# Layer 0 of a two-layer transformer kernel: a second place for queries and keys in transit, and one experts' product to a slot

## The chip, the core and the metric

The kernel runs on one core of one Trainium2 chip. The core has a matrix engine (TensorE, PE in the profile, with its weight loads shown apart as PEld), a vector engine (VectorE, DVE), a scalar engine (ScalarE, ACT), a general engine (GpSimd, POOL), and a queue for transfers (SyncE, SP). Each engine runs its own instructions in the order in which the program has them and waits for the others through semaphores. The metric is the device time of one execution in microseconds (us). The kernel before took 1177.23 us, the median of three runs (1175.32 to 1181.05).

## The reference, cut to what matters

Four sub-layers follow one another on 2048 tokens of width 256, each as `x = x + f(layernorm(x))`, all in float32.

```python
def _L0_attn_ref(x, w_project, w_out):        # 16 heads of 16, 4 sequences of 512, causal
    q, k, v = ...                             # einsum('bsd,od->bso', x, w_project)
    att = softmax(where(causal, -1e9, q @ k.T / 4))
    return einsum('bsd,od->bso', att @ v, w_out)

def _L0_ffn_ref(h, router_w, router_b, expert_w, expert_b):
    logits = (h @ router_w.T + router_b).reshape(T, O, E)         # O = 256, E = 8
    w, sel = top_k(softmax(logits), 2);  w = w / sum(w)
    c = zeros((T, E)).at[t_idx, sel].add(w)                       # 256 choices fall on 8 experts
    expert_out = einsum('th,eoh->teo', h, expert_w) + expert_b
    return einsum('te,teo->to', c, expert_out)
```

The second layer has an attention with 16 heads of 128 over the sequences' position in the batch, and a gated network of width 2048 with 4-bit weights. For this change the experts' layer is the part to keep in mind: per group of 128 tokens it needs four products of 128x256 by 256x512 for the router (the logits), then a long chain on DVE that turns the logits into the eight weights `c` of each token, and then four products of the same size with the experts' matrices (the results), which ACT scales by `c` and DVE adds up. There are 16 groups, so 64 logit products and 64 result products.

## The kernel before

Tokens are cut into 16 groups of 128, four groups to a block (`NBLK` = 4). Layer 0's attention runs over the blocks in turn, because of the causal mask: block j sees the keys of blocks 0 to j. Its work is cut into 44 batches (`batches`, filled at the head of the attention): 4 batches for block 0, 8 for block 1, 16 for block 2 and 16 for block 3. A batch n does, on PE: the scores of the next batch (`greatest`, L647), the transpose of the row maxima (`shift`, L676), a mask (`mask`, L660), then the product with the values for the batch before (`mixed`, L731) and the scores once more, transposed (`powers`, L695), for the exponentials on ACT. DVE takes the maxima (L666) and subtracts them from the queries (L679).

All instructions of PE, DVE, ACT and POOL are in an order written by the program. Everything that isn't the attention itself is put between these steps by a small planner. A job is a generator, a `Stream`, that says before each piece what it needs: an engine, a cost in planned us, a gap in slots and a condition. A call of `fill` opens a slot. It sets what is left of each engine's budget to `min(left, 0) + budget`, so that a debt is carried on and a rest is thrown away, and then goes through the streams in order and lets each put in pieces as long as `ready` says yes. `ready` asks for `left > 0`, so a piece may overdraw the budget. Batch n has slots 2n+1 (after `mask`) and 2n+2 (after `powers`), with PE budgets of 2.0 and 2.4 for blocks 0 and 1, 1.8 and 2.2 for block 2, 1.6 and 2.0 for block 3; DVE gets 2.6 in each.

The streams that matter here, in the order in which a slot asks them:

- `prepare(j)` (j = 2, 3): normalises a block, transposes it, and runs `projections(j, xT)`: the values (cost 1.75), then for each half of the 256 query and key columns two calls of `project`, i = 0 for the keys and 1 for the queries, at 1.75 each. `project` multiplies (L545), ACT copies the product into a tile `stage` (L549), and after i = 1 eight DMAs from SP (L555) carry the stage's rows to their places in `qk`. The tile `stage` is in pool `a1`, which has one buffer for that name.
- `divided(j, s)`: the attention's division and output product (L749, L766, L778); once a block's last is done, `hidden_pieces(j)` makes the experts' normalised input `xT`.
- `addition_pieces` (DVE 1.55: adds half a group's results to the residual), `total_pieces` and `weight_pieces` (17 DVE pieces for a group, 18 planned us; when the last is done, the group enters `weights`).
- `result_pieces` and, after it, `logit_pieces`: each piece is one product, PE cost 1.85. Conditions tie them to `made()`, the number of groups whose 17 DVE pieces are done, in fractions: logit g, pair p waits for `made() >= g - 0.9 + 0.22 p` and for the weights of group g - 2; result h, pair p for `made() >= h + 1 + 0.22 p` or for no logits waiting. The third and fourth product of a group wait until the sum of the first two has been added.

The experts' tiles are in pools with one buffer per name (`b1`): among them `hi4` and `lo4` (the weights' chain) and `part` (a half group's scaled results). Before the first group's chain starts, `hi4` holds the biases as they were loaded (`bs`), and `part` holds what the biases are folded in with (`rows`, last read by the fold at L252).

What of the experts' work is left at the end of layer 0's attention goes on in layer 1's attention. There 16 steps p (block j, key head kv) have nine slots each. Until step 8 (`LAST`), a step gets `share = products_left / (9 * (LAST + 1 - p))`, and its slots have a PE budget of `1.9 * share + 0.2` and a DVE budget of `2.7 * share + 1.4`. From step 9 on `share` is 0. Ahead of step 10 a loop of slots (PE 2.0, DVE 3.0) runs until the last sum is added; from step 10 the 4-bit weights of layer 1's gate and up matrices are unpacked in the space that this frees (`weight_in_pieces`, L878 to L905).

Of the kernel before, what the change touches and what calls it, by code (L numbers as in the profile page):

```python
# [8 lines left out]
F32 = mybir.dt.float32  # L9
# [7 lines left out]
P = 128  # L17
# [15 lines left out]
def tile_transformer(  # L33
# [71 lines left out]
    b1 = w_ffn0.enter_context(tc.tile_pool(name="f0_1", bufs=1, side="right"))  # L105
# [6 lines left out]
    slot = 0  # L112

    def need(engine, cost, gap=0, cond=None):
        return engine, cost, gap, cond

    class Stream:
# [4 lines left out]
        def ready(self, left):  # L122
            if self.next is None:
                return False
            engine, cost, gap, cond = self.next
            return left[engine] > 0 and slot >= self.last + gap and (cond is None or cond())

        def go(self):
            engine, cost = self.next[:2]
# [17 lines left out]
    left = {"PE": 0.0, "DVE": 0.0}  # L147
# [113 lines left out]
    logits, weights, halves = {}, {}, {}  # L261
# [187 lines left out]
    with ExitStack() as l0:  # L449
# [90 lines left out]
        def project(j, xT, half, stage, i):  # L540

            at = 256 * (1 - i) + 128 * half
            ps = ps_dn.tile([P, 512], F32, tag="dn", name=f"qk_ps{j}_{half}_{i}")
            for hc in range(2):
                nc.tensor.matmul(  # L545
                    ps, lhsT=wp[:, hc, at : at + P],
                    rhs=xT[:, hc].rearrange("p s q -> p (s q)"), start=hc == 0, stop=hc == 1,
                )
            nc.scalar.copy(stage[:, i], ps)  # L549
            if i:  # L550
                to = 4 + j % 2
                for r in range(8):
                    h = 32 * (r % 4)
                    eng = nc.scalar if j == 0 and r % 2 else nc.sync
                    eng.dma_start(  # L555
                        out=qk[h + 4 : h + 20, 2 * half + r // 4, j : to + 1 : to - j].rearrange(
                            "p i s q -> p i (s q)"
                        ),
                        in_=stage[16 * r : 16 * r + 16],
                    )  # L560

        def values(j, xT, s):

            ps = ps_dn.tile([P, 2, HID], F32, tag="dn", name=f"v_ps{j}_{s}")
            for i in range(2):
                for hc in range(2):
                    nc.tensor.matmul(
                        ps[:, i], lhsT=xT[:, hc, s + i], rhs=wp[:, hc, 512:768],
                        start=hc == 0, stop=hc == 1,
                    )  # L570
            at = j * per_block
            to = va[:, at : at + per_block].rearrange("p (s h d) -> p s h d", s=NS, d=17)
            nc.scalar.copy(
                to[:, s : s + 2, :, 0:16], ps.rearrange("p s (h d) -> p s h d", d=16)
            )
# [14 lines left out]
        def projections(j, xT):  # L590
            if j > 1:
                for s in (0, 2):
                    yield need("PE", 1.75, 1, cond=lambda: blanked > 5 * j - 10)
                    values(j, xT, s)
            for half in range(2):
                if j or half:
                    stage = a1.tile([P, 2, 512], F32, tag="stage", name=f"stage{j}_{half}")
                else:
                    stage = unused("stage0", "p (i q) -> p i q", i=2)
                for i in range(2):  # L600

                    yield need(
                        "PE", 1.75, 0 if half or i else 1,
                        cond=lambda: j < 2 or done >= 8 * j - 12 and blanked >= 5 * j - 5,
                    )
                    project(j, xT, half, stage, i)
                if half == (not j) and j < 2:
                    for s in (0, 2):
                        yield need("PE", 1.75)
                        values(j, xT, s)  # L610

        def prepare(j):

            out = []
            yield from norm_pieces(
                j, b1, b2, out, cond=lambda: j == 2 or inputs[2].next is None
            )
            xT = a1.tile([P, 2, NS, P], F32, tag="xT0", name=f"xT0_{j}")
            yield from inputs_T(j, out[0], xT)
            yield from projections(j, xT)  # L620

        def unused(name, pattern, **sizes):

            tile = b2.tile([P, NE, HID], F32, tag="lg", name=name)
            return tile.rearrange("p e o -> p (e o)")[:, :1024].rearrange(pattern, **sizes)
# [188 lines left out]
        for piece in projections(0, xT):  # L814
            pass
# [3 lines left out]
        greatest(0)  # L819
        mask(0)  # L820
        inputs = {1: Stream(projections(1, xT))}
        done = blanked = 0
        fold = Stream(fold_pieces())
# [4 lines left out]
        for n in range(NBT):  # L828
            j, s, gs = batches[n]
# [92 lines left out]
    with ExitStack() as l1:  # L922
# [198 lines left out]
        for p in range(-1, NP):  # L1121
            j, kv = divmod(p, NKV)
# [179 lines left out]
```

## Time and profile before

| | |
|---|---|
| median of the runs | 1177.23 us |
| the profiled execution, its own time | 1182.05 us |
| its span, first to last instruction | 1180.3 us |
| PE, PEld, DVE, ACT, POOL busy | 1148.1, 663.9, 809.7, 484.3, 108.1 us |
| layer 0's attention, from the first batch to the last | about 31 to 404 us |
| layer 1's attention | about 404 to 840 us |
| the gated network | about 840 to 1180 us |

A row of the timeline has the start of an instruction (or of several alike in a row), its length, engine and line, what it writes and reads, its shape, and in brackets how long the engine was idle ahead of it and who ended that. A row of the windows has the length of a stretch and then the busy time and the number of instructions of each engine in it, the clock that was granted to TensorE as a share of full speed, the share of the DMA engines' time and GB/s. Matmuls are pipelined, and the end of each is modelled, so two that follow one another overlap in the rows: four matmuls of 128x512 are shown with 0.59 us each but start 0.43 us apart, and a product takes 1.72 us from its start to the next.

### The profile page before, as it was taken

How to read it: one execution, taken by the hardware profiler on the slowest of the kernel's cores; microseconds unless marked ns; L12 is line 12 of the kernel's file. 1: busy time of each engine (PE TensorE's matmuls, PEld its weight loads, DVE VectorE, ACT ScalarE, POOL GpSimd, SP SyncE). 2: the span in 40 equal slices, each digit the busy share in tenths (PEclk: the TensorE clock that was granted, in tenths of full speed). 3: DMA queues.
4: the chain of work that ended last, by engine and by line, in shares of the span. 5: the costliest groups of instructions: out<-in, count | busy, mean ns of one | idle time of the engine just before them, and what ended most of it. 6: DMA issues, size and time to landing. Idle time of an engine off the chain costs nothing.

```text
span 1180.3 us, 18580 instructions
## 1 busy us (share of the span) xinstructions
PE 1148.1 (97%) x7178; PEld 663.9 (56%) x7178; DVE 809.7 (69%) x1783; ACT 484.3 (41%) x1099; POOL 108.1 (9%) x152
## 2 busy tenths in 40 slices
PE   7999989999999899999999999999999999999998
PEld 3656545555555445555555556565644465485487
DVE  5656869999989872867872685687599844725710
ACT  1434545555565453444444443555244312303300
POOL 7313212111111100000000000000000000000000
PEclk9989989999999999999999999999999999999999
DMA  7320010000000320000000001020020000000000
GB/s 217 68 67 12 10 28 1 1 1 2 2 1 2 113 66 1 1 1 1 1 1 1 1 1 45 19 58 24 21 50 3 0 1 18 0 1 18 1 13 23
DMA packets 21239, 26.46 MB, mean 22 GB/s; under 512 B 5128, under 2 KB 14600, under 8 KB 21152
## 3 DMA queue, kind: packets, MB, share of 16 engines
q1 hardware_dynamic: 20480, 24.10, 7.6%
q10 hardware_dynamic: 672, 1.18, 0.4%
q8 instruction: 56, 0.92, 0.3%
q14 instruction: 31, 0.25, 0.1%
HBM read 18.97 MB, written 2.10 MB: 18 GB/s over the span
## 4 chain that ended last, share of the span: by engine, by line
PE 79%; DVE 15%; ACT 2%; issue 2%; POOL 1%; DMA 1%; SPq 0%; ACTq 0%; DVEq 0%; POOLq 0%
PE qk_ps L982 11%; PE y L1229 9%; PE o L1073 9%; PE g L911 9%; PE u L911 9%; PE lg_ps L234 8%; PE eo L234 7%; DVE mx L666 3%; PE s L647 3%; PE s L695 3%; PE av L731 2%; PE qk_ps L545 2%; PE v_ps L964 2%; PE a L1053 1%; PE s L995 1%
## 5 line engine op out<-in xcount | busy, mean ns | idle before, releaser
L982 PE MATMUL qk_ps<-xT,wqkv 128*128 128x512 f32 x320 | 148.9, 599 | 2.3 <-ACT part L323 1.2
L234 PE MATMUL lg_ps<-rw,xT 128*128 128x512 f32 x256 | 122.5, 601 | 1.3 <-ACT xT L949 0.3
L234 PE MATMUL eo<-ew,xT 128*128 128x512 f32 x256 | 121.5, 600 | 0.8 <-ACT lg L297 0.5
L1073 PE MATMUL o<-wpj,oT 128*128 128x256 f32 x512 | 119.1, 382 | 0.0
L1229 PE MATMUL y<-wd,it 128*128 128x256 f32 x512 | 111.8, 379 | 0.0
L1073 PEld LDWEIGHTS o<-wpj,oT 128*128 128x128 f32 x512 | 95.9, 190 | 27.5 <-issue 14.3
L1229 PEld LDWEIGHTS y<-wd,it 128*128 128x128 f32 x512 | 97.0, 190 | 15.0 <-issue 2.2
L666 DVE TENSOR_REDUCE mx<-s 128x1 f32<-128x384 f32 (+3 forms) x176 | 100.4, 631 | 1.4 <-PE s L660 1.4
L982 PEld LDWEIGHTS qk_ps<-xT,wqkv 128*128 128x128 f32 x320 | 59.1, 190 | 71.4 <-issue 57.4
L704 ACT ACTIVATE pt<-s 128x512 f32<-128x512 f32 (+1 forms) x176 | 84.1, 564 | 36.3 <-PE s L695 36.3
L911 PE MATMUL g<-xT,wgu 128*128 128x512 f32 x192 | 90.4, 593 | 0.0
L911 PE MATMUL u<-xT,wgu 128*128 128x512 f32 x192 | 90.2, 592 | 0.0
L323 ACT ACTIVATE part<-eo,c 128x256 f32<-128x256 f32 x128 | 53.6, 472 | 84.7 <-PE eo L234 77.1
L714 POOL TENSOR_SCALAR_AFFINE_SELECT pt<-pt 128x256 f32<-128x256 f32 (+2 forms) x88 | 62.8, 720 | 261.9 <-ACT pt L704 261.3
L1207 ACT ACTIVATE th<-sq 128x512 f32<-128x512 f32 x64 | 40.3, 630 | 87.6 <-DVE sq L1206 87.6
L234 PEld LDWEIGHTS lg_ps<-rw,xT 128*128 128x128 f32 x256 | 46.1, 190 | 46.1 <-issue 37.3
L234 PEld LDWEIGHTS eo<-ew,xT 128*128 128x128 f32 x256 | 46.1, 190 | 45.7 <-issue 38.3
L222 DVE TENSOR_TENSOR xres<-xres,y 128x256 f32<-128x256 f32 x16 | 6.7, 421 | 92.5 <-PE y L1229 92.5
L185 POOL TENSOR_TENSOR ln_rs<-rs_v,minus_half 128x4 f32<-128x4 f32 x16 | 17.6, 1100 | 552.2 <-DVE rs_v L184 439.8
L297 ACT COPY lg<-lg_ps 128x512 f32<-128x512 f32 x64 | 37.6, 588 | 73.5 <-PE lg_ps L234 73.5
L1208 DVE SCALAR_TENSOR_TENSOR th<-th,g 128x512 f32<-128x512 f32 x63 | 43.1, 684 | 29.3 <-ACT th L1207 29.2
L911 PEld LDWEIGHTS u<-xT,wgu 128*128 128x128 f32 x192 | 36.5, 190 | 45.9 <-issue 44.7
(233 smaller groups left out, 1784.4 us busy)
## 6 DMA issues: line engine op xcount, KB each, us to landing
qk<-stage SPq DMA_DIRECT2D x56, 64.0 KB, 2.4
wqkv<-in_w_qkv SPq DMA_DIRECT2D x8, 320.0 KB, 6.6
rw<-in_router_w SPq DMA_DIRECT2D x8, 256.0 KB, 6.9
ew<-in_expert_w SPq DMA_DIRECT2D x8, 256.0 KB, 5.0
wpj<-in_w_proj SPq DMA_DIRECT2D x1, 2048.0 KB
out<-xres SPq DMA_DIRECT2D x4, 512.0 KB, 2.6
xres<-in_x SPq DMA_DIRECT2D x3, 512.0 KB, 8.5
dq_wgu<-in_gate_w SPq DMA_DIRECT2D x8, 128.0 KB, 2.4
```

The source lines that it names most:

```text
L234: nc.tensor.matmul(ps, lhsT=xT[:, hc, (g % 4) * P : (g % 4 + 1) * P], rhs=w[:, hc, 2 * pair : 2 * pair + 2, :].rearrange("p e o -> p (e o) ...
L297: nc.scalar.copy(lg[:, 2 * pair : 2 * pair + 2, :].rearrange("p e o -> p (e o)"), ps)
L323: nc.scalar.mul(part[:, e % 4], ps[:, i], c[:, e : e + 1])
L666: nc.vector.tensor_reduce(maxes[n % 2][:, h, gs[0] : gs[0] + nb], ps[:, : nb * nk].rearrange("p (b k) -> p b k", b=nb), AX.X, ALU.max,)
L704: nc.scalar.activation(pt[:, i, : nb * nk], tiles[2 * pair + i][:, : nb * nk], AF.Exp, scale=0.25)
L714: nc.gpsimd.affine_select(out=last, in_=last, compare_op=ALU.is_ge, fill=0.0, base=0, pattern=pattern, channel_multiplier=-1,)
L911: nc.tensor.matmul(ps, lhsT=wgu[:, w, half, jj, par * P : (par + 1) * P], rhs=xT[:, half, :], start=half == 0, stop=half == 1,)
L982: nc.tensor.matmul(ps, lhsT=wqkv[:, hc, kv, h, :], rhs=xT[:, hc, :], start=hc == 0, stop=hc == 1,)
L1073: nc.tensor.matmul(ys[t // 2][:, t % 2], lhsT=state["o"][:, h, t * P : (t + 1) * P], rhs=wpj[:, HPK * kv + h, :], start=kv == 0 and h == 0 ...
L1207: nc.scalar.activation(th, sq, AF.Tanh, scale=0.7978845608028654)
L1208: nc.vector.scalar_tensor_tensor(th, th, 1.0, gp, ALU.add, ALU.mult)
L1229: nc.tensor.matmul(ps, lhsT=it[:, c // 2, c % 2, t * P : (t + 1) * P], rhs=wd[:, c // 2, c % 2, :], start=c == 0, stop=c == 2 * NJ - 1,)
```

## The change

It has two parts. First, for blocks 2 and 3, the second half of the queries and keys gets another tile to wait in than the first half: for block 2 the tile `hi4`, for block 3 the tile `part`, both in the experts' pool `b1`. Blocks 0 and 1 are as before. Second, `ready` asks for more of a budget for the experts' products. They are the pieces with a PE cost over 1.8; as soon as any group is in `weights`, such a piece needs more than half of its cost, 0.925, where any rest over 0 was enough. All other pieces, and the products before that, are as before. No instruction of an engine is added or taken away.

```diff
             engine, cost, gap, cond = self.next
-            return left[engine] > 0 and slot >= self.last + gap and (cond is None or cond())
+
+            least = cost / 2 if engine == "PE" and cost > 1.8 and weights else 0.0
+            return left[engine] > least and slot >= self.last + gap and (cond is None or cond())
...
             for half in range(2):
-                if j or half:
+                if j > 1 and half:
+
+                    stage = b1.tile(
+                        [P, 2, 512], F32, tag="hi4" if j == 2 else "part", name=f"stage{j}_1"
+                    )
+                elif j or half:
                     stage = a1.tile([P, 2, 512], F32, tag="stage", name=f"stage{j}_{half}")
                 else:
                     stage = unused("stage0", "p (i q) -> p i q", i=2)
```

## The prediction

> **What bounds the kernel now.** I read the page first, then the list of who waited for whom, the timeline around the longest waits, and windows over parts of the kernel.
>
> ```profile
> span 1180.3 us, 18580 instructions
> ...
> PE 1148.1 (97%) x7178; PEld 663.9 (56%) x7178; DVE 809.7 (69%) x1783; ACT 484.3 (41%) x1099; POOL 108.1 (9%) x152
> ...
> PEclk9989989999999999999999999999999999999999
> ```
>
> PE is the bound: 97% busy, and 79% of the chain that ended last. The clock row shows a slice at 8 tenths, the third, and another, the sixth: something happens to PE near 70 and 160 us. The list of waits has it:
>
> ```profile
> ACT stage L549 <- DMA qk<-stage: 12.1, 3, 4.7
> ...
> PE qk_ps L545 <- ACT stage L549: 6.0, 2, 3.2
> ```
>
> Three times ACT stands before a copy into `stage` until DMAs have read the tile's earlier contents, 12.1 us together, and twice PE then waits for ACT. The timeline of one of them (start, length, engine and line):
>
> ```profile
> 67.82 0.33 PE L676 MATMUL mxT<-ident,mx 128*128 128x128 f32 x1
> 71.21 19.89 SPq L555 DMA_DIRECT2D qk<-stage  x16
> 71.68 1.17 PE L695 MATMUL s<-qk 32*128 32x128 f32 x32
> 73.28 1.88 PE L545 MATMUL qk_ps<-xT,wp 128*128 128x512 f32 x4
> 76.38 0.33 PE L676 MATMUL mxT<-ident,mx 128*128 128x128 f32 x1
> 79.57 0.59 ACT L549 COPY stage<-qk_ps 128x512 f32<-128x512 f32 x1 [4.58 <-DMA qk<-stage]
> 80.21 3.78 PE L545 MATMUL qk_ps<-xT,wp 128*128 128x512 f32 x4 [2.85 <-ACT stage L549]
> 86.21 1.18 PE L695 MATMUL s<-qk 32*128 32x128 f32 x32
> ```
>
> This is block 2. The keys of its second half are multiplied at 73.28, but their copy has to wait until 79.57 for the eight DMAs of the first half. The queries' product needs the PSUM buffer that this copy frees, and starts at 80.21. It then takes 3.78 us instead of 1.88: the clock has dropped.
>
> ```profile
> 78.00:80.00 2.00, 0.00 (x0) 0.00 (x0) 1.56 (x3) 0.43 (x1) 0.00 (x0) 0.86 0.21 37
> 82.00:84.00 2.00, 2.00 (x4) 0.49 (x2) 0.00 (x0) 0.00 (x0) 0.00 (x0) 0.50 0.00 0
> 86.00:88.00 2.00, 2.00 (x43) 1.62 (x36) 0.00 (x0) 0.90 (x3) 0.00 (x0) 0.93 0.53 89
> ```
>
> (Busy times of PE, PEld, DVE, ACT, POOL; then the clock.) DVE is idle from 80 to 84: in this stretch everything waits for PE. Block 3's turn, at 148 us, looks alike: ACT waits 4.71, PE 3.20, the clock is at 0.50 from 152 to 158, and DVE idles 10.86 us until the next maxima arrive. The third wait (2.77 us at 20 us) is block 0's, which the change leaves alone.
>
> In layer 1's attention PE has no slack at all. Two steps, from one score to the next (L995):
>
> ```profile
> 611.74:643.47 31.73, 31.73 (x149) 17.59 (x148) 11.50 (x35) 14.04 (x38) 0.00 (x0) 1.00 0.00 1
> 791.60:809.61 18.01, 18.01 (x118) 11.43 (x117) 15.45 (x26) 9.52 (x14) 0.00 (x0) 1.00 0.21 54
> ```
>
> **Part 1, the second tile.** The copy no longer waits for DMAs. What is late next? `hi4` held the biases, last read by POOL at 22.5 us; `part` held the fold's rows, last read by PE at 89.2; the copies come at 75 and 147, so no new wait stands before them. ACT can copy when the keys are done, about 75.4, so the buffer is free before PE has done its transposes at 77.4, and PE goes straight on. The maxima that free the next scores' buffers end at 79.56; PE needs them only after the product (1.72), a bias fold and the values' step (1.0), at about 80.3. So PE itself is next, and the batch should look like the one before, which holds the same pieces: from L676 to L695 71.68 - 67.82 = 3.86 us instead of 86.21 - 76.38 = 9.83. **Saved: 5.97.** Block 3: the batch before takes 140.44 to 143.71, 3.27 us, and this one 147.75 to 156.88, 9.13, with a transpose pair of 0.38 more: 5.48 saved. Its second half (156.88 to 162.75, 5.87) has an output product and a logit product; the next batch's has only the output product and takes 3.66 (165.80 to 169.46), so 3.66 + 1.72 = 5.38 was due and 0.49 more comes back. **Saved: 5.97.** Together **11.9 us**. Nothing on DVE takes it back: it idles 10.86 us there, about 5 after.
>
> Who comes to use the tiles next? `hi4` is written by DVE for the first group at about 128.5, and block 2's DMAs are done by 94. `part` is written by ACT at 171.8; the second half's DMAs, eight at 0.6 us on SP and 2.4 to land, end at about 159 if the copies run at 151, and that ACT instruction moves to about 160. The margin is 1 us; if it is missed, ACT loses that 1 us, with the products' other PSUM buffer still free. I cost it at 0.
>
> [...] The rows show 0.50 for about 6 us after each gap, worth some 3 us each, which with the idling is the 11.9. I go by the rows.
>
> **Part 2, one product to a slot.** No work goes away; products move. I followed the plan on paper from slot 28, with the costs and conditions of the code. Slot 46 shows the rule: -0.25 + 2.2 = 1.95, a result leaves 0.10. Before, a logit followed (debt 1.75); now 0.10 is too little, it is thrown away and the logit comes in slot 47. In block 2 this only pairs 3 + 1 products in two batches as 2 + 2: by slot 56 both plans have 96 left. In block 3 the budgets are 1.6 and 2.0: a debt over 0.675 now forbids a product in a slot of 1.6 (slot 59: -0.60 + 1.6 - 0.3 = 0.70). My plan loses products in slots 59, 67, 69, 73, 77, 83; at the end of layer 0's attention (slot 95) **68 products are left instead of 64**, and five DVE pieces of 0.68 (L423 and L426) go with them.
>
> What does layer 0 win? In block 2 the batches, from one L676 to the next, take 5.07 with no product, 6.22 and 6.44 with one, 7.09 and 7.37 with two, 8.41 and 8.63 with three: 1.15 for each. In block 3 they take 7.35 with two and 7.51 with one: nothing, DVE has 36 of 40 us there. So four products less give between 0 and 4.6; I take 3, near the DVE pieces' 3.4. The evening out: 8.41 + 6.22 = 14.63 and 8.63 + 6.44 = 15.07 against 7.09 + 7.37 = 14.46, so 0.2 and 0.6: 0.8.
>
> What does layer 1 pay? [...] But the rows above answer: 31.73 with eight products, 18.01 with none, (31.73 - 18.01) / 8 = 1.715, a product's full time. So 4 x 1.72 = **6.9 us more**.
>
> The end of the experts. My plan has 59, 56, 50, 42, 35, 28, 23, 17 and 10 products left after steps -1 to 7. In step 8 the last logit falls in its second slot, the last weights in its ninth, and 4 results stay over, where before slots with two finished all. Budgets of step 9 are too small, so the loop ahead of step 10 puts in the four and two sums. These four are among the products counted; PE loses at most some tenths waiting for ACT. Layer 1's last block is normalised in step 10 instead of 9 and still needs the three extra slots of step 11. The 4-bit loads (716 us before) wait for that loop; SP needs 0.46 us for each of 18 DMAs, 8 us, and DVE may stand so long at the first, ahead of a softmax that is 12 us away: hidden. If not, up to 5 us. Unpacking ends nine slots ahead of the end instead of eleven. On the other side, PE's 1.23 us at 696 (ACT with a result that waits for its weights, behind two products in one slot) go. Part 2: 6.9 - 3 - 0.8 - 1.2 = **+1.9**, between -2 and +8.
>
> **Sum.** -11.9 + 1.9 = -10.0 us. The profiled execution took 1182.05 (1.75 outside its span), 0.4% over the median; the same difference from there gives 1172, and from the median of the runs 1177.2 - 10.0 = **1167.2**.
>
> **Rivals.** *The win is half* (0.14): another wait takes the copy's place, the maxima or POOL's mask ahead of L731, and PE still stands for 3 us at either place, so that the clock drops as now. Left: about half of 11.9; with part 2, 1177.2 - 6 + 2 = 1173. For it: L731 waits for DVE 17.5 us in all; against: by the batch before, these are ready. *The experts end late* (0.12), the slower side: the last group's logits come so late that the weights are not made when the loop of step 10 begins. There is nothing else to emit there, ACT stands at a result for its weights, PE behind ACT. Price: a group's 17 pieces on DVE, about 16 us by their rows (4 x 1.24, 2.8, 2.1, 0.3 for the small one, 8 x 0.68), 3 of clock, and some unpacking pushed into the gated network, where DVE has 38.6 of 40: 5. Then 1177.2 - 10 + 24 = 1191; with half the chain left, 1181. It decides when the last logit is over 4 slots later than my plan has it: step 9 gives DVE only 1.4 a slot. For it: 68 products instead of 64 and one a slot; against: `share` grows with what is left. *Smoothing is worth more* (0.10): layer 0 follows PE throughout and takes 1.15 off for each product moved, and the waits at 376 to 394 (3.6 us) shrink: 1162.
>
> The forecast itself has 0.64. A measurement tells 0.5% from nothing, 5.9 us: faster is below 1171.3. Faster: 0.62 of the forecast's cases and the smoothing's 0.10, 0.72 in all; same: 0.02 of the forecast, the half win's 0.13, 0.15; slower 0.13. The costs' ends (6 to 12 for part 1, -2 to +8 for part 2) give 1163 to 1173 for the forecast; the range that holds eight in ten reaches to the half win and a mild late end: 1161 to 1177.
>
> **What would show it.** No wait of ACT for `qk<-stage` but block 0's; the clock row without its eights; L676 to L695 under 4.2 us in the batches near 76 and 145; steps of layer 1 at 18.0 + 1.72 for each product; four results in a row ahead of step 10. I am wrong if PE still idles 3 us there, or if DVE's weights chain is seen with PE standing near 740 us.

## The result, and the profile after

| | before | after |
|---|---|---|
| median of the runs | 1177.14 us (1175.32 to 1181.05) | 1186.27 us (1184.43 to 1186.91) |
| profiled execution: time, span | 1182.05, 1180.3 | 1185.89, 1184.2 |

The ratio is 1.0073, with a 95% interval of 1.005 to 1.0096: the change made the kernel slower by 0.7%, where 0.8% less time was forecast. This is the page of the kernel after. Its lines stand 2 to 7 further down than before: L549 is now L551, L676 is L683, L695 is L702, L995 is L1002.

```profile
span 1184.2 us, 18553 instructions
...
PE 1145.4 (97%) x7178; PEld 662.8 (56%) x7178; DVE 807.4 (68%) x1783; ACT 484.3 (41%) x1099; POOL 104.9 (9%) x152
...
PEclk9999999999999899999999999999999999999999
```

PE is busy for 2.7 us less in a span that is 3.9 us longer, so it stands more. The two early eights of the clock row are gone, as forecast, but there is a new one further on, in the slice from 385 to 414 us. First the place that the second tile was for, block 2's second half, in the timeline:

```profile
75.78 0.59 ACT L551 COPY stage<-qk_ps 128x512 f32<-128x512 f32 x1 [0.20 <-PE qk_ps L547]
...
76.97 0.33 PE L683 MATMUL mxT<-ident,mx 128*128 128x128 f32 x1
...
77.79 1.88 PE L547 MATMUL qk_ps<-xT,wp 128*128 128x512 f32 x4
...
80.83 1.17 PE L702 MATMUL s<-qk 32*128 32x128 f32 x32
```

ACT copies the keys at once (0.20 us of waiting for PE, where it was 4.58 for DMAs), the queries' product starts at 77.79 instead of 80.21 and takes 1.88 instead of 3.78, and from L683 to L702 it is 3.86 us, the figure of the forecast to the hundredth. The first part did what it was to do. The loss must lie in the second.

### The profile page after: what moved, and what is told of

It is laid out like the page before. It is cut to its first block, busy times and chain, and to the rows that moved or that the text cites. A ratio compares the mean times of both kernels' runs of the same rounds, so it can differ in the third digit from the quotient of the medians.

```text
span 1184.2 us, 18553 instructions
## 1 busy us (share of the span) xinstructions
PE 1145.4 (97%) x7178; PEld 662.8 (56%) x7178; DVE 807.4 (68%) x1783; ACT 484.3 (41%) x1099; POOL 104.9 (9%) x152
## 3 DMA queue, kind: packets, MB, share of 16 engines
q10 hardware_dynamic: 672, 1.18, 0.4%
## 4 chain that ended last, share of the span: by engine, by line
PE 80%; DVE 14%; ACT 2%; issue 1%; POOL 1%; DMA 1%; SPq 1%; DVEq 0%; ACTq 0%; POOLq 0%
PE qk_ps L989 10%; PE y L1236 9%; PE g L918 9%; PE u L918 9%; PE o L1080 8%; PE lg_ps L236 8%; PE eo L236 7%; PE s L654 4%; PE s L702 3%; PE av L738 3%; PE v_ps L971 2%; DVE mx L673 2%; PE qk_ps L547 2%; PE a L1060 1%; PE s L1002 1%
## 5 line engine op out<-in xcount | busy, mean ns | idle before, releaser
L721 POOL TENSOR_SCALAR_AFFINE_SELECT pt<-pt 128x256 f32<-128x256 f32 (+2 forms) x88 | 58.5, 670 | 241.4 <-ACT pt L711 241.0
L352 DVE TENSOR_TENSOR part<-part 128x512 f32<-128x512 f32 x32 | 22.3, 698 | 68.4 <-ACT part L325 68.4
```

The costliest lines, as they stand in the source:

```text
L721: nc.gpsimd.affine_select(out=last, in_=last, compare_op=ALU.is_ge, fill=0.0, base=0, pattern=pattern, channel_multiplier=-1,)
```

## The experiments

**The parts alone.** First, each part without the other: the theory that the rule costs more than the tile wins, against the rival that both are harmless alone and meet somewhere. The tile alone leaves `ready` as it was:

```diff
-            least = cost / 2 if engine == "PE" and cost > 1.8 and weights else 0.0
-            return left[engine] > least and slot >= self.last + gap and (cond is None or cond())
+            return left[engine] > 0 and slot >= self.last + gap and (cond is None or cond())
```

> The second tile alone, products as before. Theory A (the tile gains what was forecast, the rule loses all of it and more, and the two don't depend on one another): the two waits go as in the changed kernel, 11.8 us, the plan is that of before, so about 1165 us, ratio 0.990; steps 8 to 10 of layer 1 as before (26.6, 24.9, 22.0 us). Theory B (layer 0 ending earlier, or the experts' tiles being lent out, makes the later collisions): the gain comes at 76 and 145 us and is lost again by 760 us, 1175 to 1185.

Measured: 1170.07 us, ratio 0.9932 (0.9916 to 0.9949); here and below the ratio is to the kernel before, measured beside the run. The time is 5 us above the 1165 of theory A, and steps 8 to 10 are as expected. A second measurement at the end, to compare with the last runs, had this expectation:

> The second tile alone, once more, beside the versions that are to beat it. By the earlier run 1170.1 us, 0.993 of the time before; nothing else differs, so within 2 us of that.

It gave 1169.82 us, ratio 0.9921 (0.9907 to 0.9934). The rule alone leaves out the hunk with the second tile:

> The rule on the products alone, stage as before. Theory A: the changed kernel's time plus the two waits, 1186 + 12 = 1198 us, ratio 1.018; idle PE at the end of layer 0's attention, near 710 and near 755 as in the changed kernel. Theory B: without the early end of layer 0 the collisions stay away, about 1180.

Measured: 1194.33 us, ratio 1.0144 (1.0121 to 1.0167). The two parts add up: the tile wins 8.3 us (1178.38 of the kernel before, beside it, - 1170.07), the rule costs 16.2 beside the tile (1186.27 - 1170.07) and 16.0 without it (1194.33 - 1178.38). Neither changes what the other does.

**Where the rule's 16 us are.** The tile alone is the right kernel to set the changed one against, since only the rule differs. The table has the starts of the transpose of the last batch of layer 0 (L683), and of the scores s0 to s15 of layer 1 (L1002), read from the two timelines. Layer 1's steps stayed at 18.0 us and 1.72 for each product, so the products in a stretch say what is due. Both kernels have 13 products between the last batch and s0.

| stretch | tile alone | after | difference | due to products | rest |
|---|---|---|---|---|---|
| start to the last batch | 366.50 | 358.72 | -7.8 | 4 fewer | -7.8 |
| last batch to s0 | 53.00 | 59.00 | +6.0 | 0 | +6.0 |
| s0 to s9 | 270.81 | 274.68 | +3.9 | 2 more: +3.4 | +0.4 |
| s9 to s10 | 24.87 | 29.74 | +4.9 | 2 fewer: -3.4 | +8.3 |
| s10 to s13 | 64.90 | 73.32 | +8.4 | 4 more: +6.9 | +1.5 |

The rest of the kernel takes the same time to a few hundredths. The sum, 15.4, is the difference of the spans (1184.2 - 1168.8). So four products moved to layer 1 for 6.9 us, as forecast, and won 7.8 in layer 0, more than forecast. What was not in the forecast is the 6.0 at the end of layer 0 and the 8.3 of step 9. The timeline of the changed kernel at the first of these:

```profile
380.52 0.43 DVE L388 TENSOR_TENSOR gap<-gap,m 128x256 f32<-128x256 f32 x1
380.98 0.42 ACT L392 ACTIVATE th<-gap 128x256 f32<-128x256 f32 x1 [4.15 <-DVE gap L388]
...
381.84 0.82 ACT L325 ACTIVATE part<-eo,c 128x256 f32<-128x256 f32 x2
382.71 1.98 PE L236 MATMUL lg_ps<-rw,xT 128*128 128x512 f32 x4 [1.78 <-ACT part L325]
...
385.37 0.66 PE L212 MATMUL xT_ps<-ident,xn 128*128 128x128 f32 x4 [0.24 <-ACT lg L299]
...
387.46 0.42 ACT L417 ACTIVATE spare<-owing 128x256 bf16<-128x256 f32 x1 [1.33 <-DVE owing L428]
...
388.55 1.05 ACT L956 COPY xT<-xT_ps 128x512 f32<-128x512 f32 x2
...
389.17 3.78 PE L236 MATMUL eo<-ew,xT 128*128 128x512 f32 x4 [3.14 <-ACT xT L956]
```

Read it from the brackets back. PE's product at 389.17 needs a PSUM buffer that ACT's copy at 388.55 frees. The transposes for that copy were done at 386. ACT could not come to it, because four sums of the weights' chain (L417) stand ahead of it in ACT's order, and each waits for a DVE instruction that goes before it. The sum at 387.46 has waited 1.33 us for DVE's L428. PE stood for 3.14 us, and its product then took 3.78 instead of 1.88, at a clock of 0.50 (window 388 to 392). Step 9 has the same thing twice over (DVE's chain first, then ACT and PE):

```profile
689.68 1.23 DVE L373 TENSOR_TENSOR hi<-lg 128x1024 f32<-128x1024 f32 x1 [1.57 <-ACT lg L299]
...
696.91 2.35 DVE L399 TENSOR_TENSOR lg<-lg,m 128x1024 f32<-128x1024 f32 x2
699.18 0.71 DVE L1011 STREAM_TRANSPOSE sm<-s 128x512 f32<-128x512 f32 x1
...
701.89 0.26 ACT L1030 ACTIVATE ex<-sc 128x64 f32<-128x64 f32 x1 [10.52 <-DVE sc L1023]
...
703.77 1.98 PE L989 MATMUL qk_ps<-xT,wqkv 128*128 128x512 f32 x4 [1.48 <-ACT part L325]
...
707.87 0.42 ACT L417 ACTIVATE spare<-owing 128x256 bf16<-128x256 f32 x1 [0.17 <-DVE owing L428]
...
708.29 0.82 ACT L325 ACTIVATE part<-eo,c 128x256 f32<-128x256 f32 x2
...
709.16 3.78 PE L989 MATMUL qk_ps<-xT,wqkv 128*128 128x512 f32 x4 [3.41 <-ACT part L325]
```

The last group's logits are complete just ahead of the score of step 9, in slots of step 8 whose DVE budget is 4.4. So the first part of its chain, 9.5 us from 689.68 on, stands in DVE's order ahead of the softmax, whose first instruction (L1011) comes at 699.18 though its score was done at 693.5. ACT stands 10.52 us at the softmax's exponential with the experts' results behind it (1.48 of PE's time), and after it with the sums (3.41). The clock in the windows from 708 to 716 is 0.56 and 0.59.

In the tile alone, the same two places look like this:

```profile
391.66 0.17 DVE L437 SCALAR_TENSOR_TENSOR c<-sums,c 128x8 f32<-128x8 f32 x1
...
394.07 0.59 ACT L954 COPY xT<-xT_ps 128x512 f32<-128x512 f32 x1
...
690.31 1.08 PE L1000 MATMUL s<-qT,kT 128*32 128x128 f32 x32 [0.18 <-ACT kT L991]
...
691.71 0.17 DVE L437 SCALAR_TENSOR_TENSOR c<-sums,c 128x8 f32<-128x8 f32 x1
691.79 0.71 DVE L1009 STREAM_TRANSPOSE sm<-s 128x512 f32<-128x512 f32 x1
```

L437 is the last instruction of a group's chain. At the end of layer 0 it is done before the copy L954 comes, so no sum stands ahead of that. In step 9 the last group's chain ends 1.4 us after the score has started (in the changed kernel 19.4 us after it, at 711.80), and the softmax begins as soon as its score is done.

**The rule in one layer alone.** Is the price paid by the products that layer 0 hands on, or by the rule in layer 1? A flag switches the rule off where layer 1's first stream starts; in the other run it is off until there and is switched on:

```diff
-            least = cost / 2 if engine == "PE" and cost > 1.8 and weights else 0.0
+            least = cost / 2 if engine == "PE" and cost > 1.8 and weights and spaced[0] else 0.0
...
+        spaced[0] = False
         inputs = Stream(start_pieces(0))
```

> Both parts, but the rule holds only until layer 1's attention starts; from there a product needs a rest over 0 again. The plan has 69 products left at layer 1's start as in the changed kernel, and 1 instead of 4 ahead of step 10. Theory A1 (the loss is made in layer 1, by the last group's chain in step 8 and by the four late results): steps 8 to 10 lose their 11 us of standing PE, about 1176. Theory A2 (the loss is made by what layer 0 hands over: five products and a late chain at its end): still slow, 1182 to 1186.

> Both parts, but the rule holds only from the start of layer 1's attention. Layer 0 is planned as before (64 products left), 4 results are left ahead of step 10 as in the changed kernel. Theory A1: the standing of PE in steps 8 to 10 is there, 6 to 11 us over the tile alone, 1171 to 1177. Theory A2: close to the tile alone, 1165 to 1168.

Measured: 1178.85 us (ratio 1.0006, 0.9997 to 1.0016) with the rule in layer 0 alone, 1177.52 (0.9994, 0.9986 to 1.0003) in layer 1 alone. Against the tile alone that is 8.8 and 7.4. That these add up to 16.2 is no division of the changed kernel's loss, since the losses stand at other places than there. By the stretches of the table, with 1.72 for each product, the rule in layer 0 alone has nothing left over in step 9, but 1.7 ahead of s0, 4.9 from s0 to s9 (a wait of 2.74 for ACT's `part` in step 0, and behind it a product of 3.03 us at 427.71, where one at 421.26 takes 1.98) and 3.1 from s10 to s13. The rule in layer 1 alone has 4.9 ahead of s0, 1.2 from s0 to s9, 0.6 in step 9 and 2.6 from s10 to s13, so most of it is not in steps 8 to 10, where theory A1 had it. In the 4.9, PE stands behind ACT once more, 1.18 and 2.26 us for copies of `v`, the second of which comes behind six sums that each wait for DVE; the two products behind that (406.45 and 409.01) take 2.77 and 2.83 us, where one at 411.68 takes 1.88.

One thing does follow. The run in layer 1 alone hands on no product (64 are left when layer 1 starts, as with the tile alone), and still loses 7.4 us. So moved products can't be the whole price.

**Undoing one standing place at a time.** In the changed kernel, step 9 may take the products that are left (`share` 1 instead of 0):

```diff
             share = products_left / (9 * (LAST + 1 - p)) if p <= LAST else 0.0
+            if p == LAST + 1:
+                share = 1.0 if products_left else 0.0
```

> The changed kernel, but step 9 of layer 1 gets a share of 1 while products are left, so that the four late results fall in step 9 and the loop ahead of step 10 has nothing to do. Theory L (the late loads: unpacking starts before its weights have landed, DVE stands 2.8 us, ACT behind it, PE behind ACT): step 10 loses its 2.7 us of standing PE, about 1183, and step 9's standing near 705 stays. If the late results cost only their own products, nothing moves: 1186.

Or the score and the first part of the softmax of step 9 are put ahead of the slot that holds the chain:

```diff
                 if not t and new:
+                    if p == LAST:
+                        score(p + 1)
+                        softmax_1(p + 1)
+                        between()
+                        continue
                     between()
                     score(p + 1)
                 elif t == 1 and new:
-                    softmax_1(p + 1)
+                    if p != LAST:
+                        softmax_1(p + 1)
```

> The changed kernel, but in step 8 the softmax of the next step is put ahead of the slot that carries the second lot of the last group's chain, so that DVE has it about 5 us earlier; all else as it is. Theory S (the last group's chain, nine us of it in two slots, stands in front of the softmax; ACT waits at its exponential, and PE for the products that ACT holds): the interval of step 9, 29.7 us where its two products and the step's own work take 21.4, falls to 22 to 24, the clock stays up, about 1179. If instead ACT waits for the weights of the results, the standing stays: 1186.

Or ACT's sums of the group whose chain runs when layer 1 starts are put off by three slots instead of one, so that ACT copies first:

```diff
-                defer(sum_up, last=slot % 2 == 1)
+                defer(sum_up, 3 if entering[0] else 1, last=slot % 2 == 1)
...
+        entering[0], entered = True, slot
...
             fill(PE=2.0, DVE=3.0)
+            entering[0] = slot < entered + 2
```

> The changed kernel, but the sums on ACT of two slots at the start of layer 1 are put two slots later, behind the copies of layer 1's first transposed input. Theory C (these sums wait for DVE's chain, which comes later than before, and hold the copies that PE needs at 389 us): PE's wait of 3.1 us there goes, and with it the drop of the clock; the first score of layer 1 comes 3 to 5 us earlier, about 1182. If the chain on DVE holds PE in another way, through the transposes or through PSUM, less than 1 us.

Measured: 1184.32, 1185.0 and 1179.91 us (ratios 1.0045, 1.005 and 1.0008). Only the last does much, 6.4 us. With step 9 taking the products, the wait of 2.66 in step 10 for ACT's `qT` goes as expected, but PE now waits 1.99 us there for DVE's normalisation of the last block (`xn`), with the clock at 0.50 behind it (window 737 to 740), and only 2.0 us are won. For the last of the three, the timeline at the end of layer 0:

```profile
386.42 1.06 ACT L957 COPY xT<-xT_ps 128x512 f32<-128x512 f32 x2
387.05 1.98 PE L237 MATMUL eo<-ew,xT 128*128 128x512 f32 x4 [0.62 <-ACT xT L957]
...
391.26 0.42 ACT L418 ACTIVATE spare<-owing 128x256 bf16<-128x256 f32 x1
```

The copy no longer stands behind waiting sums, PE waits 0.62 instead of 3.14, the clock stays at 1.00 (windows from 376 to 400), and the stretch takes 53.89 us, against 59.00 and the 53.00 of the tile alone.

The softmax put first missed: PE's two waits of step 9 became one of 4.74 us, since the sums, which wait for DVE, still stood ahead of ACT's `part`:

```profile
701.66 0.42 ACT L417 ACTIVATE spare<-owing__6707 128x256 bf16<-128x256 f32 x1 [3.37 <-DVE sums L411]
...
705.74 3.78 PE L989 MATMUL qk_ps<-xT,wqkv 128*128 128x512 f32 x4 [4.74 <-ACT part L325]
```

To change the order on DVE alone was not enough. All three together:

> The changed kernel with the three edits of e6, e7 and e8 together. If the three places are independent and are what the rule loses beside the products that it moves, 1186 - 3 - 7 - 4 = 1172 us, close to the tile alone (1170), because the rule's win in layer 0's batches (7.8 us in the traces) is about what its four products cost in layer 1 (6.9).

Measured: 1182.61 us (1.003, 1.0019 to 1.0041), 2.7 worse than the sums alone. In its trace, step 9 again has one wait of 4.73, with the clock at 0.50 in the window from 704 to 708, and the steps 9 and 10 take 61.62 us together, against 58.11 with the sums alone. The edits don't add up: the softmax put first makes one long gap of two (4.74 us alone, with the clock at 0.55 from 704 to 708), and the sums that hold up ACT are still ahead of `part`.

**The last group's sums.** The deciding run mends ACT's order in step 9 as well: to the sums put off at layer 1's start, the last group's are added, and no product moves.

```diff
-                defer(sum_up, 3 if entering[0] else 1, last=slot % 2 == 1)
+                defer(sum_up, 3 if entering[0] or g == NT - 1 else 1, last=slot % 2 == 1)
```

> The changed kernel with ScalarE's sums put off by three slots instead of one at layer 1's start (as in the run before) and for the last group too. The products stand in the same slots, four of them still ahead of step 10. If PE stands in step 9 because the copies that it needs queue on ScalarE behind the last group's sums: the waits of 1.47 and 3.40 us for ScalarE at the projections of step 9 fall under 1 us together, the step takes about 22 us instead of 26.8 to 29.7, the clock stays at 1.00 there, and the time is 1173 to 1177. If the four late products themselves are what is paid and the waits only go elsewhere: 1178 to 1181, as with the sums put off at layer 1's start alone (1179.9).

Measured: 1175.8 us, ratio 0.9971 (0.996 to 0.9982). In its timeline of step 9 the second wait is gone:

```profile
699.30 3.70 PE L990 MATMUL qk_ps<-xT,wqkv 128*128 128x512 f32 x8 [1.48 <-ACT part L326]
...
703.04 0.59 ACT L994 COPY qT<-qk_ps 128x512 f32<-128x512 f32 x1 [1.13 <-PE qk_ps L990]
703.52 0.42 ACT L418 ACTIVATE spare<-owing__6707 128x256 bf16<-128x256 f32 x1
...
704.03 5.42 PE L990 MATMUL qk_ps<-xT,wqkv 128*128 128x512 f32 x12
```

The projections at 704.03 follow without a wait, behind copies that stand ahead of the sums now, and the step takes 23.18 us instead of 29.74. With ACT's order mended at both places, 10.5 of the 16.2 us are back (1186.27 - 1175.8) with every product in its slot. The time is in the expected range. The 1.48 should have shrunk too, and stayed: it comes from the exponential's wait, which is 10.52 us here as well.

**The late products.** What is left is about 6 us, and the trace of this last run shows where. Against the tile alone, its batches of layer 0 win 7.7 and the four moved products cost 6.9, so these two cancel. Over the products, it has 0.9 more between the last batch and s0, 1.0 from s0 to s9, 1.7 in step 9 and 3.0 from s10 to s13, which makes the 5.8 between the two spans (1174.6 - 1168.8). The largest piece is step 10. In the changed kernel:

```profile
743.13 0.43 DVE L897 TENSOR_SCALAR dq_mgu<-dq_wgu 128x512 int32<-128x512 int32 x1 [2.80 <-DMA dq_wgu<-in_up_w]
...
744.01 1.15 ACT L899 ACTIVATE dq_bgu<-dq_mgu,minus 128x1024 f32<-128x1024 int32 x1 [4.12 <-DVE dq_mgu L898]
745.07 1.05 ACT L1066 COPY oT<-a 128x512 f32<-128x512 f32 x2
...
746.66 0.66 PE L212 MATMUL xT_ps<-ident,xn 128*128 128x128 f32 x4 [2.66 <-ACT qT L993]
```

The chain is the same again: DVE waits for the 4-bit weights, which are loaded only when the last result is added, ACT waits for DVE with copies behind it, PE waits for ACT. Two runs, with the flag set at each batch so that the rule holds in blocks 0 to 2 of layer 0 only, test it apart. In the first, two results stay ahead of step 10; the second has the lines of `share` too, so that step 9 takes them:

```diff
+            spaced[0] = j < 3
...
             share = products_left / (9 * (LAST + 1 - p)) if p <= LAST else 0.0
+            if p == LAST + 1:
+                share = 1.0 if products_left else 0.0
```

> Both parts, the rule of one product to a slot only for the batches of layer 0's blocks 0 to 2. Two more products than with the tile alone go into layer 1 (66 instead of 64 are left there after its first step), and two are left ahead of step 10. If a product that leaves layer 0 costs layer 1 its full 1.72 us and wins about as much in block 2: the last batch of layer 0 starts some 3 us earlier, the end of the experts takes it back with about 3 to 5 us, 1169 to 1174. If the evening out of block 2 is worth more than the two products: 1165 to 1168.

> The same as the run with the rule for blocks 0 to 2, and step 9 takes the products that are left (a budget of 2.1 for PE and 4.1 for DVE instead of 0.2 and 1.4), so that none stands ahead of step 10. If the late results hold up the 4-bit loads and the last layer's unpacking: step 10 is back at about 22 us and the time 2 to 4 us below that of the run without this. If the two products only move from one step to the other: the same time within 1 us.

Measured: 1179.2 us (0.9999, 0.999 to 1.0007) and 1175.64 us (0.9972, 0.996 to 0.9984). In step 10 of the first, the chain is that of the changed kernel: DVE waits 2.82 us for the weights, ACT 4.50 for DVE, PE 3.04 for ACT. Without late results this wait of PE is gone, and the time falls by 3.6: the late loads are not hidden. (The second run also brings the normalisation of layer 1's last block forward by a step, so the 3.6 are those of the late results as a whole.) From s9 to s13 it is 5.9 us less (93.79 and 87.85, with four products in each), part of which is lost again at other places. The other expectation missed: both are well above the tile alone, though only three more products were handed on. Their last batch starts about 7 us earlier than with the tile alone (at 359.74 and 358.93 instead of 366.50), but a new wait of 4.2 us for ACT's copy L958 stands in step 0 (at 439.95 in the second), with the clock at 0.50 behind it (window 440 to 443), and 1.80 for a load of `wqkv` ahead of s0. The copy stands behind four sums (L418) that each wait for DVE, as at the end of layer 0 in the changed kernel.

None of these versions beats the tile alone at 1169.82 us.

## Why the prediction was wrong

**The second tile** was right in its mechanism. In the traces it takes 11.5 us off the span (1180.3 - 1168.8), against 11.9 forecast, and no other wait came in its place. Its size in the timed runs is 8.3 and 8.9. The term of the clock (3 us for each gap) was taken from one profiled execution, in which the clock was at 0.50 for 6.83 us at each gap (79.45 to 86.27 and 151.13 to 157.95). In the run of the rule alone, where two such gaps remain (2.68 and 2.95 us, where they were 2.85 and 3.20), the two batches take 12.65 and 13.38 us instead of 14.16 and 15.00. The product behind each gap takes 3.50 and 2.40 us, where it took 3.78 both times, and the clock is back at 1.00 in the window from 84 to 86, which has 0.50 in the profile before. The timed runs show it too. Of the 24 of the kernel before in the last measurement, the fastest (1175.66 us) has a mean clock of 0.999 and the slowest (1182.81) of 0.993. The drops are not of one size in all executions, and a sum set against a median should not have counted them in full. The 17.5 us at L731, which the rival of half the win had for itself, are in the list of waits those of PEld, the weight loads, and not of PE.

**Products to layer 1: 6.9** was right, to the number of products: four ahead of step 10, four in a row there from 728.44, 1.72 each.

**Layer 0's win** of 3 + 0.8 was too small, 7.8 by the table. The mis-sized term is the evening out, 0.8. In block 2 the batches are 5.0 us faster than with the tile alone, of which one product that leaves there may be 1.15 by the forecast's own price; in block 3, where the other three leave, they are 2.6 faster, near the 3 that were forecast. The pairs that the forecast summed, 8.41 + 6.22 and 8.63 + 6.44, became 6.70 + 6.70 and 7.12 + 6.91 (the second with one product fewer), which is 1.2 and 1.0 less, and not 0.2 and 0.6: it had taken batches with two products from before (7.09 and 7.37) as the measure, and there were quicker ones to come. The other 2.8 us of block 2 are in batches that the forecast did not sum.

**The end of the experts** is the step that failed: "PE loses at most some tenths waiting for ACT", and of the later loads "hidden. If not, up to 5 us". Its plan had the last logit and the four late results in the right slots. But it followed budgets, and not the orders of ACT and DVE, and so missed what the slots did: the first 9.5 us of the last group's chain, put ahead of a softmax; ACT, in order behind it; and PE behind ACT. It cost 8.3 in step 9 (waits of 1.48 and 3.41, and the clock) and 1.5 in step 10 and after. There the loads were not hidden: what stood next behind ACT's part of the unpacking was not the softmax, 12 us away, but copies that PE needed, and PE stood for 2.66 us. The 1.2 that the forecast had on the other side, PE's wait at 696, did go, but a wait of 1.86 for ACT's `part` came in step 0.

**The end of layer 0** was not costed at all: the working goes from the batches straight to layer 1's steps, though the plan moves products in the slots between them as well. There ACT's copy stood behind four sums, PE stood for 3.14 us and the clock fell to 0.50, and this took back 6.0 of the 7.8. The rival of the smoothing had these waits shrink; they grew.

With these, the rule's part is -7.8 + 6.0 + 6.9 + 8.3 + 1.5 + 0.4 = +15.3 in the traces (15.4 before rounding), where +1.9 was forecast. The late rival had the right side and a range that holds the measured time (1181 to 1191), but by luck, since its mechanism is not what happened: weights were ready when the loop of step 10 began, and nothing stood near 740 for want of them. What decided was where the chain fell in the engines' orders, not how late it was. That two changes of ACT's order alone give 10.5 us back is shown. Where the other 5.7 us stand is shown too, with 3.0 from s10 to s13 and 1.7 in step 9 as the largest. What causes them is shown only in part: the late results with their loads cost 3.6 us in another pair of runs, and a wait of 1.48 stays in step 9. A kernel that mends these too, with the sums put off, was not run.

## What to carry to other kernels

When work is moved between engines' in-order programs, cost the orders, not the budgets (here two changes of ACT's order alone gave 10.5 us back): for each moved piece, write down which copies and exponentials stand behind it on ACT and DVE, and whether PE waits for one of them. A filler that waits (a sum that needs the instruction before it on another engine) should be issued late enough for its input to be there, behind the copies on which the matrix engine depends. And try the parts of a change alone: here one part was worth 0.7% and the other cost twice that.

## What was not expected of the hardware

Equal gaps of PE had unequal effects on its clock. A wait of 3.41 us in step 9 is followed by these windows in the changed kernel:

```profile
708.00:712.00 4.00, 2.84 (x4) 1.17 (x4) 3.86 (x16) 2.78 (x11) 0.00 (x0) 0.56 0.00 0
712.00:716.00 4.00, 4.00 (x36) 2.46 (x35) 0.00 (x0) 1.61 (x3) 0.00 (x0) 0.59 0.00 0
```

and the same wait, 3.40 us ending at 704.41, by these where only layer 1's first sums were put off:

```profile
704.00:708.00 4.00, 3.59 (x38) 2.00 (x39) 3.11 (x13) 3.10 (x11) 0.00 (x0) 1.00 0.00 0
708.00:712.00 4.00, 4.00 (x11) 1.85 (x10) 0.00 (x0) 2.50 (x6) 0.00 (x0) 1.00 0.00 0
```

The third figure from the end is the granted clock. The step takes 29.74 us in the one and 26.84 in the other, with the same products, so the drop alone is 2.9 us. (With the rule alone, where the product behind this wait takes 1.98 us and not 3.78, the step takes 26.85.)

The end of layer 0 shows three outcomes of one wait. It is 3.14 to 3.16 us in four traces, with the same products around it. Behind it the clock is at 0.50 for 6.83 us in the changed kernel (387.61 to 394.44), and the product there takes 3.78 us. With the rule alone that product takes 3.38 us (at 398.07), and the four behind it 7.03, so the clock is up again sooner. In the two runs that mend step 9 by its share or its softmax the product takes 1.98 and 1.99 us, with the clock at 1.00 in the window from 388 to 392. The stretch from the last batch to s0 takes 59.00, 57.82, 56.40 and 56.39 us. So some 2.6 of the 6.0 us lost there are the clock's, and are not lost in every execution. A product was also slow where PE had hardly stood before: in the second measurement of the tile alone (mean clock 0.999, in the first 1.000) a logit product takes 3.49 us at 191.89, where in the first measurement the same one takes 1.94, and the longest wait of PE in the rows of the 5 us before it is 0.16. The two batches around it take the same together, 15.72 and 15.75 us.

Ten of the traces have a wait of 1.98 to 3.04 us in step 10. In seven of them the clock falls to between 0.50 and 0.71 in a window of 3 us behind it (with 1.99 us: 0.50; 2.65: 0.54; 3.04: 0.50). In one, the rule alone, the product behind a wait of 2.67 us takes 3.68 (at 752.44), where the one before it takes 1.85 on the mean. In two the clock stays at 1.00 (2.66 in the changed kernel, 2.69 with the softmax put first). Both waits of 4.7 us that were seen lowered it (0.50 and 0.55 in the windows from 704 to 708). What decides between the outcomes is not shown by any run here. In these runs a gap of 2 to 3.4 us was a chance of losing up to some 3 us more (2.9 in step 9, 2.6 at the end of layer 0), not a fixed price.
